# The time mix's residual: added by VectorE from SBUF, instead of by TensorE in PSUM

## The chip, the cores and the metric

The kernel runs on one core of one Trainium2 chip. The time is that of the device, in microseconds (us), as the median of several runs. TensorE multiplies matrices into PSUM, VectorE, ScalarE and GpSimd work element by element, and SyncE (SP) issues the transfers; GpSimd has only tiles in SBUF to work on here. The profile shortens the names: PE is TensorE, PEld its weight loads, DVE VectorE, ACT ScalarE, POOL GpSimd.

## The reference, cut to what matters

Sixteen sequences of 512 tokens with 128 features go through four layers, each with its residual and a layer norm behind it: a recurrent block (time mix and channel mix), a tree of soft decisions, a causal attention with 16 heads of 8, and a mixture of 16 experts of which each token uses two. The change lies in the first block:

```python
x = _ln(x, ln0_g, ln0_b)
xn = _ln(x, pre_g, pre_b)
...
rwkv = jax.nn.sigmoid(r) * (wkv / (wk + K_EPS))
x = x + rwkv @ tm_Wo
xn = _ln(x, post_g, post_b)
...
x = x + (jax.nn.sigmoid(xr @ cm_Wr) + kv)
```

Everything behind the block is a layer norm, so the kernel may keep x centred (its mean over the features taken away).

## The kernel before, in words

A tile is 128 features by 512 tokens in f32: one sequence ("batch"), with the features on the partitions. Means over the features are products with constant matrices: `centre` takes the mean away, `mean_w` gives the mean of the squares. A norm is thus a product with `centre`, a square on ScalarE, a product with `mean_w`, a logarithm and an exponential on ScalarE (together the power -1/2, called r), and one multiplication.

For each batch b, `front(b)` goes from the input to the tensors of the attention. It centres x0 into a PSUM bank (p0). x1 is p0 times g and r, on VectorE, without the bias b of the first norm. A second bank, p1, takes `centre` x x1 and then the centred bias: `b0p` (three bf16 parts of the bias, made in `prepare_mixes`) times a row of ones. `shifted_norm` squares p1, makes r, and writes xn from p1 and r on VectorE; dx is the difference of neighbouring tokens (GpSimd), xx the shifted copy (ScalarE), and three mixes of them follow on VectorE. Four `rwkv` chunks then run the recurrence (scans and a reciprocal on VectorE, products on GpSimd) and leave `rw`. The bank p2 takes `centre` x x1 and the bias rows once more, and over them the four products of `tm_o` and `rw`: that is the new residual x2. ScalarE copies p2 to SBUF as x2 (the tile `y`), while `shifted_norm` reads p2 itself. Then follow the channel mix (`hidden`), the bank p3, the tree (`gates`, `lp`), the rotation for the attention (tile `four`, event "rot") and the transfer out of the parts.

Beside the fronts run long pieces that go through all batches: `operands` (transfers), `greatest` (scores `sc` and their greatest value on VectorE, then small steps on GpSimd), `weighted` (scores `st`, exponentials on ScalarE), `sums` (`o`), `ends`, `gating`, `by_gate` (`us`: products with the gates on GpSimd), `experts` (`acc`) and `output`.

All instructions are written out by a planner, the class `Plan`. Each piece is a generator; the planner keeps a clock and a cost for each engine, and when an engine is free it takes the waiting piece with the smallest (time of asking + slack). The tables `S_FRONT`, `S_RWKV` and so on hold these slacks for TensorE (PE), VectorE (V), ScalarE (A) and GpSimd (G): the larger the number, the later the piece's turn. The order that comes out is each engine's program; on the chip the engines only wait for data and for buffers. `front(b)` starts behind the events "summed" of batch b-1, "mixed" and "normed" of batch b-2, and not before `PERIOD * b - LEAD`. x2 of batch b stands behind "rot" of batch b-1. `W` is VectorE too, at a cost in the plan that grows while GpSimd is busy; `V` is VectorE at the plain cost. PSUM has eight banks, which `bank` takes and `give` returns.

Since nearly all instructions are issued in one helper, the profile shows them under one line, L219, and they are told apart by the names of tiles: `p` is p0 to p3, `x` is x0 and x1, `y` is x2 and later tensors.

Of the kernel before, what the change touches and what calls it, by code (L numbers as in the profile page):

```python
# [18 lines left out]
NC4 = 4  # L19
# [21 lines left out]
HAND_OVER = 0.2  # L41
BANKS = 8
SCORES = 5
PERIOD = 100.0

S_FRONT = {"PE": -6.0, "V": -6.0, "A": 0.0, "G": -20.0}
S_RWKV = {"PE": -10.0, "V": 15.0, "A": -10.0, "G": 6.0}
S_GREATEST = {"PE": -30.0, "V": -3.0, "A": -3.0, "G": -30.0}
S_WEIGHTED = {"PE": -20.0, "A": 30.0, "G": -15.0}
S_SUMS = {"PE": 15.0}  # L50
S_ENDS = {"PE": 6.0, "V": -6.0, "A": 50.0, "G": -15.0}
S_GATE = {"PE": -20.0, "V": 6.0, "A": 6.0, "G": 0.0}
S_EXPERTS = {"PE": 20.0}
FREE = {}
LEAD = 60.0
RWKV_PACE = 5.0
EXPERT_PACE = 0.0
MAX_PACE = 0.0
EXP_PACE = 0.0

# [197 lines left out]
def rwkv_tree_attn_moe(ctx: ExitStack, tc: tile.TileContext, a: dict, out: bass.AP):  # L258
# [54 lines left out]
    def fixed(name, shape, dtype=F32):  # L313
        return const.tile(shape, dtype, tag=name, name=name)
# [25 lines left out]
    def col(i):  # L340
        return vec[:, i:i + 1]
# [23 lines left out]
        if scale != 1.0:  # L365
            V.tensor_scalar(w, w, scale, None, ALU.mult)

    ones, b0p, minus = fixed("ones", [PARTS, T], BF16), fixed("b0p", [PARTS, D], BF16), fixed("minus", [128, 2])
    decay, first = fixed("decay", [128, NC4]), fixed("first", [128, NC4])

    def prepare_mixes():

        V.memset(ones, 1.0)
        b0 = pp.tile([128, PARTS], F32, tag="b0", name="b0")
        for i in range(PARTS):
            V.tensor_copy(b0[:, i:i + 1], col(V_LN0B))
        yield
        p = yield from bank("p_b0")
        mm(p[0:PARTS, 0:D], b0, centre, start=True, stop=True)

        act(decay, vec[:, V_DECAY:V_DECAY + 4], AF.Exp)
        act(decay, decay, AF.Exp, scale=-1.0)
        act(first, vec[:, V_FIRST:V_FIRST + 4], AF.Exp)

        V.tensor_scalar(minus[:, 0:1], col(V_PREB), -1.0, None, ALU.mult)
        V.tensor_scalar(minus[:, 1:2], col(V_POSTB), -1.0, None, ALU.mult)
        yield
        b0r = pp.tile([PARTS, D], F32, tag="b0r", name="b0r")
        V.tensor_copy(b0r, p[0:PARTS, 0:D])
        give(p)  # L390
        b0m = pp.tile([PARTS, D], BF16, tag="b0m", name="b0m")
        for i in range(PARTS):
            V.tensor_copy(b0m, b0r)
            V.tensor_tensor(b0r, b0r, b0m, ALU.subtract)
            if i == 0:
                V.tensor_scalar(b0p, b0m, ident[0:PARTS, 0:1], None, ALU.mult)
            else:
                V.scalar_tensor_tensor(b0p, b0m, ident[0:PARTS, i:i + 1], b0p, ALU.mult, ALU.add)
        event("mixes").set()
        yield 12.0  # L400
        centred(tm_o, 0.5)
        centred(cm_v, 0.5)
        event("outputs").set()
# [131 lines left out]
    def give(p):  # L535
        banks.put(held.pop(id(p))[1])
# [17 lines left out]
        act(r, r, AF.Exp, scale=-0.5)  # L554
        return r

    def variance(d, tag):

        sq = t512(tag)
        act(sq, d, AF.Square)  # L560
        yield
        pv = yield from bank("pv")
        mm(pv, mean_w, sq, start=True, stop=True)
        yield
        return pv

    def normed(d, tag, to):
        pv = yield from variance(d, tag)
        r = rstd_of(pv, ln_eps, to)
        give(pv)  # L570
        yield
        return r

    def front(b, keep):
# [16 lines left out]
        give(p)  # L591
        yield

        def shifted_norm(p, g, minus_b, b):

            r = yield from normed(p, sq, rr)
            shift = yield shifts
            xn = pp.tile([128, T + 1], F32, tag="xn", name="xn")
            G.tensor_copy(xn[:, 0:1], minus_b)
            V.scalar_tensor_tensor(xn[:, 1:T + 1], p, g, r, ALU.mult, ALU.mult)  # L600
            give(p)
            yield
            dx, xx = t512("dx"), t512("xx")
            act(xx, xn[:, 0:T], AF.Identity, bias=b)
            G.tensor_tensor(dx, xn[:, 1:T + 1], xn[:, 0:T], ALU.subtract)
            yield
            return dx, xx, shift
# [5 lines left out]

        yield event("mixes")
        p = yield from bank("p1")
        mm(p, centre, x1, start=True, stop=False)
        mm(p, b0p, ones, start=False, stop=True)
        yield
        dx, xx, shift = yield from shifted_norm(p, col(V_PREG), minus[:, 0:1], col(V_PREB))
        xk, xr, xv = mix(dx, xx, V_MK, "xk"), mix(dx, xx, V_MR, "xr"), mix(dx, xx, V_MV, "xv")  # L620
        shifts.put(shift)
        yield
# [48 lines left out]
        yield event("outputs")  # L671
        yield event("rw", b, 0)
        p = yield from bank("p2")
        mm(p, centre, x1, start=True, stop=False)
        mm(p, b0p, ones, start=False, stop=False)
        event("x1", b).set()
        for c in range(NC4):
            yield event("rw", b, c)
            mm(p, tm_o[:, c, :], rw[:, c, :], start=False, stop=(c == NC4 - 1))
        event("summed", b).set()  # L680
        yield
        if b:
            yield event("rot", b - 1)
        x2 = t512("y")
        copy(x2, p)
        dx, xx, shift = yield from shifted_norm(p, col(V_POSTG), minus[:, 1:2], col(V_POSTB))
        xk, xr = mix(dx, xx, V_CMK, "ck"), mix(dx, xx, V_CMR, "cr")
        shifts.put(shift)
        yield
# [500 lines left out]
```

## Time and profile before

| | |
|---|---|
| runs | 1847.95 us median of 3 (1846.07 to 1852.24) |
| the profiled execution | 1852.02 us, span 1850.2 us |
| mean granted TensorE clock | 0.957 |
| x1 of batches 1, 4, 8, 12 and 15 written at | 82, 359, 759, 1177 and 1495 us |
| p2 of batch 12 complete, rotation of batch 11 done, x2 of batch 12 begun | 1252.5, 1276.9, 1276.1 us |
| last exponential of the attention done | about 1787 us |

A group's row gives the engine, the operation, out<-in, the shapes and the count; then the busy time in us and the mean of one in ns; then the engine's idle time just before these instructions and what ended it. A row of busy time by stretch gives the stretch and its length, then for PE, PEld, DVE, ACT and POOL the busy time and the number of instructions, then the granted clock, the share of the DMA engines and GB/s. A row in order of time gives the start, the time until the end of the last of the merged instructions, and the engine; a TensorE instruction's listed end is modelled, so the start of the next one tells how long it held the engine. An f32 product of 512 columns is two records.

### The profile page before, as it was taken

The numbers are of one execution on the slowest core, as the hardware profiler recorded it, in microseconds if no ns is written. First come the engines' busy times: TensorE is split into PE (matmuls) and PEld (weight loads), VectorE is DVE, ScalarE is ACT, GpSimd is POOL, SyncE is SP. The second block draws the span as 40 slices with busy tenths as digits, with TensorE's granted clock in tenths as the row PEclk, the third lists the DMA queues.
The fourth block names the chain that finished last, engine by engine and source line by source line (L and its number), as shares of the span: only waits on it lengthen the run. The fifth ranks groups of instructions, "written<-read, shape, count | busy, mean of one in ns | idle before, by whom it ended". The sixth has DMA issues, their size and how long they took to land.

```text
span 1850.2 us, 25410 instructions
## 1 busy us (share of the span) xinstructions
PE 1667.9 (90%) x8580; PEld 784.5 (42%) x8668; DVE 1367.0 (74%) x1917; ACT 1172.0 (63%) x1974; POOL 1063.3 (57%) x1329
## 2 busy tenths in 40 slices
PE   5577889899999999899999999999899999998875
PEld 2233434344444444444444444444344444454431
DVE  7695879688888778686887788796878868555512
ACT  3345677668677576667767676767667666765440
POOL 2344544556765747566565757675666757545342
PEclk9687999899999999999999999999999999999996
DMA  3001010221413122222313132222213131233322
GB/s 103 1 6 56 20 38 27 79 79 32 132 37 112 62 91 78 66 82 73 97 46 105 62 96 78 95 67 65 74 58 116 51 107 62 61 94 111 97 80 97
DMA packets 61970, 133.78 MB, mean 72 GB/s; under 512 B 11708, under 2 KB 32974, under 8 KB 61585
## 3 DMA queue, kind: packets, MB, share of 16 engines
q1 hardware_dynamic: 61841, 132.16, 22.6%
q8 instruction: 69, 1.13, 0.2%
q14 instruction: 60, 0.49, 0.1%
HBM read 114.01 MB, written 17.31 MB: 71 GB/s over the span
## 4 chain that ended last, share of the span: by engine, by line
PE 49%; DVE 25%; POOL 11%; issue 6%; ACT 4%; DMA 2%; SPq 1%; POOLq 0%; DVEq 0%; ACTq 0%
PE acc L219 8%; PE sc L219 7%; PE st L219 6%; DVE sk L219 6%; PE o L219 5%; DVE skv L219 5%; PE p L219 5%; PE pv L219 4%; DVE nmx L219 3%; PE pr L219 2%; PE ph L219 2%; POOL us L219 2%; PE pk L219 2%; POOL lp L219 2%; PE pvv L219 2%
## 5 line engine op out<-in xcount | busy, mean ns | idle before, releaser
L219 DVE TENSOR_REDUCE nmx<-sc 128x1 f32<-128x384 f32 (+3 forms) x704 | 433.8, 634 | 195.6 <-PE sc L219 148.4
L219 ACT ACTIVATE ew<-st 128x512 f32<-128x512 f32 (+1 forms) x704 | 382.3, 556 | 252.1 <-PE st L219 248.0
L219 POOL TENSOR_TENSOR us<-u,gb 128x512 f32<-128x512 f32 x248 | 328.5, 1334 | 159.3 <-PE acc L219 83.6
L219 PE MATMUL acc<-us,w_mo 128*128 128x512 f32 x512 | 277.7, 634 | 17.0 <-POOL us L219 16.7
L219 PE MATMUL st<-qop,kop 128*128 128x512 bf16 (+1 forms) x1018 | 253.9, 304 | 18.1 <-DMA qop<-rows 8.5
L219 PE MATMUL sc<-kop,qop 128*128 128x128 bf16 x1021 | 257.4, 305 | 11.3 <-DVE nmx L219 7.5
L219 DVE RECIPROCAL sk<-sk 128x512 f32<-128x512 f32 x64 | 213.8, 3341 | 0.0
L219 PE MATMUL o<-ew,vaug 128*32 128x512 f32 (+3 forms) x2048 | 193.8, 447 | 6.6 <-ACT ew L219 3.4
L219 POOL TENSOR_TENSOR sk<-fk,sk 128x512 f32<-128x512 f32 x64 | 102.2, 1597 | 142.2 <-DVE sk L219 123.3
L219 PEld LDWEIGHTS <-qop 128*128 128x128 bf16 x1024 | 94.1, 100 | 182.8 <-issue 158.7
L219 PE MATMUL st<-idents,masks 128*128 128x128 bf16 (+2 forms) x673 | 161.7, 240 | 0.6 <-issue 0.4
L219 PE MATMUL sc<-masks,idents 128*128 128x128 bf16 (+2 forms) x656 | 154.9, 236 | 0.3 <-issue 0.2
L219 PEld LDWEIGHTS <-kop 128*128 128x128 bf16 x1024 | 91.6, 99 | 146.7 <-issue 102.5
L219 POOL TENSOR_TENSOR skv<-t,skv 128x512 f32<-128x512 f32 x64 | 81.4, 1272 | 89.1 <-DVE skv L219 84.3
L219 POOL TENSOR_TENSOR rw<-skv,sk 128x512 f32<-128x512 f32 x64 | 86.8, 1357 | 64.5 <-DVE sk L219 61.0
L219 PEld LDWEIGHTS acc<-us,w_mo 128*128 128x128 f32 x512 | 84.1, 195 | 80.7 <-issue 42.1
L219 POOL TENSOR_TENSOR lp<-gates,lp 128x8 f32<-128x8 f32 (+6 forms) x224 | 115.2, 536 | 2.7
L219 DVE TENSOR_TENSOR_SCAN skv<-decay,kv 128x511 f32<-128x511 f32 x64 | 112.7, 1761 | 0.0
L219 PEld LDWEIGHTS <-idents 128*128 128x128 bf16 x704 | 69.8, 99 | 88.8 <-issue 82.9
L219 PE MATMUL pv<-sq,mean_w 128*128 128x512 f32 x160 | 93.2, 666 | 14.3 <-ACT sq L219 13.5
L219 PE MATMUL p<-rw,w_tm 128*128 128x512 f32 x128 | 74.3, 664 | 34.9 <-POOL rw L219 34.5
L219 ACT ACTIVATE r<-pv,eps 128x512 f32<-128x512 f32 x96 | 65.9, 687 | 52.9 <-PE pv L219 30.1
(213 smaller groups left out, 3120.6 us busy)
## 6 DMA issues: line engine op xcount, KB each, us to landing
gb<-gd SPq DMA_DIRECT2D x128, 512.0 KB
qop<-there SPq DMA_DIRECT2D x576, 32.0 KB
kop<-there SPq DMA_DIRECT2D x192, 96.0 KB
there<-parts SPq DMA_DIRECT2D x32, 384.0 KB
x<-xT SPq DMA_DIRECT2D x16, 256.0 KB
out<-sqb SPq DMA_DIRECT2D x16, 256.0 KB
qop<-rows SPq DMA_DIRECT2D x192, 4.0 KB
w_mo<-w_mo SPq DMA_DIRECT2D x1, 1160.0 KB
```

The lines of the kernel that those rows point to most:

```text
L219: ins = getattr(self.engine, op)(out, *args, **kw)
```

## The change

The bias of the first norm is centred once into a column, `cb0`, in `prepare_mixes`; the row of ones, the three bf16 parts and the work that makes them go. p1 takes only `centre` x x1. ScalarE writes p1 plus `cb0` over x1 in SBUF, and the bank is given back at once; `shifted_norm` then reads x1 from SBUF. p2 takes only the four products of `tm_o` and `rw`; VectorE adds x1 to it as it writes x2, and `shifted_norm` reads x2 from SBUF. xn is now planned at the cost of `W`. The event "summed" is set behind that addition; the event "x1", for which no piece waits, goes. The planner's period, nine slacks and two paces get other values.

```diff
-PERIOD = 100.0
+PERIOD = 96.0
-S_FRONT = {"PE": -6.0, "V": -6.0, "A": 0.0, "G": -20.0}
-S_RWKV = {"PE": -10.0, "V": 15.0, "A": -10.0, "G": 6.0}
-S_GREATEST = {"PE": -30.0, "V": -3.0, "A": -3.0, "G": -30.0}
-S_WEIGHTED = {"PE": -20.0, "A": 30.0, "G": -15.0}
+S_FRONT = {"PE": -6.0, "V": -6.0, "A": 0.0, "G": 0.0}
+S_RWKV = {"PE": -10.0, "V": 20.0, "A": -30.0, "G": 6.0}
+S_GREATEST = {"PE": -30.0, "V": -3.0, "A": -3.0, "G": -3.0}
+S_WEIGHTED = {"PE": -20.0, "A": 3.0, "G": -10.0}
-S_ENDS = {"PE": 6.0, "V": -6.0, "A": 50.0, "G": -15.0}
-S_GATE = {"PE": -20.0, "V": 6.0, "A": 6.0, "G": 0.0}
+S_ENDS = {"PE": 6.0, "V": -3.0, "A": 30.0, "G": -15.0}
+S_GATE = {"PE": -20.0, "V": 6.0, "A": 6.0, "G": 30.0}
-RWKV_PACE = 5.0
-EXPERT_PACE = 0.0
+RWKV_PACE = 7.0
+EXPERT_PACE = 1.0
...
     def prepare_mixes():
-        V.memset(ones, 1.0)
-        b0 = pp.tile([128, PARTS], F32, tag="b0", name="b0")
-        for i in range(PARTS):
-            V.tensor_copy(b0[:, i:i + 1], col(V_LN0B))
-        yield
         p = yield from bank("p_b0")
-        mm(p[0:PARTS, 0:D], b0, centre, start=True, stop=True)
+        mm(p[:, 0:2], centre, vec[:, V_LN0B:V_LN0B + 2], start=True, stop=True)
...
-        b0r = pp.tile([PARTS, D], F32, tag="b0r", name="b0r")
-        V.tensor_copy(b0r, p[0:PARTS, 0:D])
+        V.tensor_copy(cb0, p[:, 0:1])
         give(p)
-        b0m = pp.tile([PARTS, D], BF16, tag="b0m", name="b0m")
-        for i in range(PARTS):
...
-    def variance(d, tag):
+    def variance(d, tag, bias=0.0):
         sq = t512(tag)
-        act(sq, d, AF.Square)
+        act(sq, d, AF.Square, bias=bias)
...
-            V.scalar_tensor_tensor(xn[:, 1:T + 1], p, g, r, ALU.mult, ALU.mult)
-            give(p)
+            W.scalar_tensor_tensor(xn[:, 1:T + 1], x, g, r, ALU.mult, ALU.mult)
...
-        mm(p, centre, x1, start=True, stop=False)
-        mm(p, b0p, ones, start=False, stop=True)
-        yield
-        dx, xx, shift = yield from shifted_norm(p, col(V_PREG), minus[:, 0:1], col(V_PREB))
+        mm(p, centre, x1, start=True, stop=True)
+        yield
+        act(x1, p, AF.Identity, bias=cb0)
+        give(p)
+        dx, xx, shift = yield from shifted_norm(x1, col(V_PREG), minus[:, 0:1], col(V_PREB))
...
         p = yield from bank("p2")
-        mm(p, centre, x1, start=True, stop=False)
-        mm(p, b0p, ones, start=False, stop=False)
-        event("x1", b).set()
         for c in range(NC4):
             yield event("rw", b, c)
-            mm(p, tm_o[:, c, :], rw[:, c, :], start=False, stop=(c == NC4 - 1))
-        event("summed", b).set()
+            mm(p, tm_o[:, c, :], rw[:, c, :], start=(c == 0), stop=(c == NC4 - 1))
         yield
         if b:
             yield event("rot", b - 1)
         x2 = t512("y")
-        copy(x2, p)
-        dx, xx, shift = yield from shifted_norm(p, col(V_POSTG), minus[:, 1:2], col(V_POSTB))
+        V.tensor_tensor(x2, p, x1, ALU.add)
+        event("summed", b).set()
+        give(p)
+        dx, xx, shift = yield from shifted_norm(x2, col(V_POSTG), minus[:, 1:2], col(V_POSTB))
```

More of the change, by code (lines that the diff above doesn't have):

```diff
@@ L366, in centred @@
             V.tensor_scalar(w, w, scale, None, ALU.mult)
-    ones, b0p, minus = fixed("ones", [PARTS, T], BF16), fixed("b0p", [PARTS, D], BF16), fixed("minus", [128, 2])
+    cb0, minus = fixed("cb0", [128, 1]), fixed("minus", [128, 2])
     decay, first = fixed("decay", [128, NC4]), fixed("first", [128, NC4])
     def prepare_mixes():
-        V.memset(ones, 1.0)
-        b0 = pp.tile([128, PARTS], F32, tag="b0", name="b0")
-        for i in range(PARTS):
-            V.tensor_copy(b0[:, i:i + 1], col(V_LN0B))
-        yield
         p = yield from bank("p_b0")
-        mm(p[0:PARTS, 0:D], b0, centre, start=True, stop=True)
+        mm(p[:, 0:2], centre, vec[:, V_LN0B:V_LN0B + 2], start=True, stop=True)
         act(decay, vec[:, V_DECAY:V_DECAY + 4], AF.Exp)
@@ L387, in prepare_mixes @@
         yield
-        b0r = pp.tile([PARTS, D], F32, tag="b0r", name="b0r")
-        V.tensor_copy(b0r, p[0:PARTS, 0:D])
+        V.tensor_copy(cb0, p[:, 0:1])
         give(p)
-        b0m = pp.tile([PARTS, D], BF16, tag="b0m", name="b0m")
-        for i in range(PARTS):
[L393 to L398, printed above, removed]
         event("mixes").set()
@@ L592, in front, with shifted_norm @@
         yield
-        def shifted_norm(p, g, minus_b, b):
-            r = yield from normed(p, sq, rr)
+        def shifted_norm(x, g, minus_b, b):
+            r = yield from normed(x, sq, rr)
             shift = yield shifts
```

## The prediction

> **What bounds the kernel now.** I read the busy shares first, then the busy time by stretch, then the chain that ended last, then TensorE in order of time, and last the groups and tiles that the change touches.
>
> ```profile
> PE 1667.9 (90%) x8580; PEld 784.5 (42%) x8668; DVE 1367.0 (74%) x1917; ACT 1172.0 (63%) x1974; POOL 1063.3 (57%) x1329
> ```
> ```profile
> 0.00:300.00 300.00, 216.57 (x763) 94.95 (x770) 226.95 (x298) 157.02 (x247) 129.34 (x182) 0.86 0.12 37
> 300.00:1500.00 1200.00, 1150.58 (x6146) 545.81 (x6209) 959.04 (x1315) 833.08 (x1410) 764.30 (x950) 0.99 0.24 76
> ```
> ```profile
> PE 49%; DVE 25%; POOL 11%; issue 6%; ACT 4%; DMA 2%; SPq 1%; POOLq 0%; DVEq 0%; ACTq 0%
> ```
>
> The mean of 90% hides three stages. From 300 to 1500 us TensorE is busy 1150.6 of 1200 us (96%) at a granted clock of 0.99, and nothing else is near: VectorE 80%, ScalarE 69%, GpSimd 64%. There TensorE is the bound. In the first 300 us it is idle for 83 us, because the first batches' chain runs through VectorE. The third stage begins when the last exponentials are done (about 1787): 60 us of short dependent steps, which the change doesn't touch. About half the last-ending chain is TensorE, in many lines. So a TensorE instruction removed after about 300 us should be worth the time until the next matmul can start, and one removed before it next to nothing.
>
> What a matmul is worth is its start-to-start step, not its listed 0.59 us, since matmuls overlap. In order of time, TensorE alone:
>
> ```profile
> 1012.41 0.22 PE L219 MATMUL st<-idents,masks 128*128 128x128 bf16 x1
> 1012.47 1.08 PE L219 MATMUL p<-x,centre 128*128 128x512 f32 x2
> 1013.48 0.39 PE L219 MATMUL p<-ones,b0p 3*128 3x512 bf16 x1
> 1013.79 0.39 PE L219 MATMUL st<-qop,kop 128*128 128x512 bf16 x1
> ```
>
> The f32 product of x1 (two records) holds the engine from 1012.47 to 1013.48, 1.01 us; the three bias rows from 1013.48 to 1013.79, 0.31 us.
>
> **The change part by part.**
>
> *Removed from TensorE.* Per batch: in p2 the centring product and the bias rows (1.01 + 0.31 = 1.32 us), in p1 the bias rows (0.31 us). After 300 us there are p2 of batches 3 to 15 and p1 of batches 4 to 15: 13 x 1.32 + 12 x 0.31 = 20.9 us. What falls before 300 us lies in TensorE's idle time and counts as nothing.
>
> *Removed at the start.* The ones memset, the copies of b0 and the splitting into three bf16 parts, some 3 us of VectorE before 11 us. The split ends at 10.75 us, when r, which x1 needs, had ended at 10.67: worth 0.1 us. Nothing.
>
> *Moved and added.* These rows price it:
>
> ```profile
> L219 ACT COPY y<-p 128x512 f32<-128x512 f32 x16 | 9.3, 581 | 17.5 <-PE p L219 17.5
> L219 ACT ACTIVATE sq<-y 128x512 f32<-128x512 f32 x16 | 10.1, 628 | 31.7 <-DVE y L219 31.7
> L219 DVE TENSOR_TENSOR att<-z,pw 128x512 f32<-128x512 f32 x16 | 10.7, 666 | 4.1 <-PE pw L219 3.7
> L219 DVE SCALAR_TENSOR_TENSOR xn<-p,vec,r 128x512 f32<-128x512 f32 x32 | 23.9, 746 | 22.8 <-ACT r L219 22.7
> ```
>
> ScalarE gains an Identity out of PSUM with a bias column (nearest row: the squares out of PSUM, 600 ns) and loses the copy of x2 (581): 16 x 0.02, nothing. Its 32 squares now read SBUF: 628 against 600, +0.9 us over the run. VectorE gains the addition of x1 to p2, one operand in PSUM and one in SBUF, as att has it: 16 x 0.67 = 10.7 us. All this lies beside a TensorE that is busy 96%: on VectorE it is 0.67 of about 103 us a batch, from 80% to 81%. Were that cover gone it would cost its full 11 us.
>
> *xn now reads SBUF twice* (x and r), in place of PSUM and SBUF. Duration ns min/median/max of tiles with two SBUF inputs:
>
> ```profile
> L219 DVE SCALAR_TENSOR_TENSOR xn<-p,vec,r x32: 737/744/753, 18.3 to 1600.6; 128x512 f32<-128x512 f32 x32
> L219 DVE SCALAR_TENSOR_TENSOR xk<-dx,vec,xx x16: 741/752/1743, 23.4 to 1508.8; 128x512 f32<-128x512 f32 x16
> L219 DVE SCALAR_TENSOR_TENSOR ck<-dx,vec,xx x16: 742/1140/2603, 79.7 to 1604.6; 128x512 f32<-128x512 f32 x16
> ```
>
> xn never exceeds 753 ns; the others reach 1743 and 2603. [...] the low end is the same 740 ns, the high end is longer by about one GpSimd product (1.27 us). By the mean of xk (1066 ns) the 32 xn cost 32 x 0.32 = 10 us[...]. [...] VectorE thus ends near 82%, still covered.
>
> *On the path of the first batches*, where latency counts: p1 loses 0.31 us, then gains the Identity (0.60) ahead of its square; p2's addition replaces a copy (+0.09); two xn at +0.32 each; two squares from SBUF (+0.06): about +1.1 us a batch, for three batches +3 us.
>
> *The moved event.* "summed" was set when p2 was complete; now it is set behind the addition, which stands behind the wait for "rot" of the batch before. The next batch's front stands behind it: its x load on SP's queue, its first product, all of its chain. For batches 12 and 13 the trace has:
>
> ```profile
> 1251.42 1.08 PE L219 MATMUL p<-rw,w_tm 128*128 128x512 f32 x2
> 1275.57 1.28 POOL L219 TENSOR_TENSOR four<-four 128x512 f32<-128x512 f32 x1
> 1276.09 0.58 ACT L219 COPY y<-p 128x512 f32<-128x512 f32 x1
> 1278.82 0.75 DVE L219 SCALAR_TENSOR_TENSOR x<-p,vec,r 128x512 f32<-128x512 f32 x1 [2.86 <-ACT r L219]
> ```
>
> p2 of batch 12 was complete at 1252.5; the rotation of batch 11 held x2 back to 1276.1; x1 of batch 13 came 2.7 us later, 6.2 us behind its own first product at 1272.67. Under the new order it comes after x2 plus 0.7 (addition), 4 (the code's pause for the load) and 6.2, so some 8 us later. From x1 to the end of p2 it takes 76 to 90 us over batches 2 to 13, about 79 in the middle, so the new loop is 11 + 79 + 1 = 91 us against a spacing of 102 to 103: it fits, with 11 us to spare, and costs nothing. The load itself was issued at 1207, 65 us ahead of its use, so its later place in SP's queue is covered too.
>
> *Slacks, paces, period.* The planner's order changes everywhere: on GpSimd the gate products go from 0 to +30 and the greatest scores from -30 to -3, on ScalarE the exponentials from +30 to +3 and the time mix from -10 to -30; TensorE's own values stay. No row prices a reordering. From below: it could recover at most the 49 us of TensorE's idle time between 300 and 1500, half of it at a guess, -25. From above: if its idle share doubled on half of that stretch, +25. I take 0, as TensorE's work is the same in any order. The period of 100 hardly binds now (the last x1 stand 102, 108 and 108 us apart: 1176.8, 1278.8, 1387.0, 1495.1), so 96 should change little.
>
> **Sum.** -20.9 + 3 + 0 = -18 us. The profiled execution took 1852.0 us (span 1850.2 and 1.8 around it), which gives 1834; the median of the runs is 4 us below it, so 1847.95 - 18 = **1830 us**.
>
> **Rivals.**
> *The order packs better too.* For: VectorE waits 148 us for sc, ScalarE 248 us for st, so buffers turn late; p1's PSUM bank is given back earlier. Against: only 49 us are to be had. At half of it, 1830 - 25 = 1805.
> *Hidden anyway.* From batch 3 on x2 starts within 2 us of the rotation of the batch before, so the loop x2 to rotation (95 to 110 us) also has the period. If its waits for VectorE, ScalarE and GpSimd set it, TensorE only idles more: the 18 us vanish, within 0.3%, 1843 to 1853. Against: alone, batch 0 needs 79 us for that loop; the rest is queueing, mostly at TensorE.
> *Slower: the loop through "summed" becomes the bound.* Place: x2, next front, time mix, p2. It decides once x1 to p2's end exceeds 91 us; batch 4 has 89.8 now, xn and the Identity add 1 to 2, and the pace of 7 between chunks may delay the last by 6. At a period of 105 instead of 103.4, 13 x 1.6 = 21 us more: 1869.
>
> **How the numbers follow.** Forecast 0.43, better packing 0.14, hidden 0.13, loop 0.30. A measurement of this kernel tells about 0.3% (5.5 us) from no change. Faster is 0.43 + 0.14 = 0.57, same 0.13, slower 0.30. The forecast's own range is 1820 to 1841. The range that leaves out 2 in 10 reaches half-way into the packing case and up to about the loop's price: 1808 to 1868.
>
> **What would show it.** TensorE's busy time falls by some 26 us (16 x 1.63), its share from 300 to 1500 stays near 96%, and fronts come some 101.8 us apart. xn spreads to a mean near 1.05 us with a top over 1.7. x1 follows x2 of the batch before by about 11 us, and p2 still ends ahead of the rotation. The forecast is wrong if TensorE's idle share in that stretch grows by over 2 points (loop or order), or if x2 now waits for p2 rather than for the rotation.

## The result, and the profile after

The changed kernel takes 1859.34 us (median of 5 runs, 1857.42 to 1860.6); the kernel before took 1846.61 us in the same comparison. The ratio is 1.0058, with a 95% interval of 1.0042 to 1.0073: slower by 0.58%, some 11 to 13 us. The forecast was 1830, with a range of 1820 to 1841.

The page of the kernel after, busy shares first:

```profile
PE 1647.7 (89%) x8604; PEld 778.8 (42%) x8604; DVE 1384.3 (75%) x1920; ACT 1180.6 (64%) x1978; POOL 1069.3 (58%) x1329
```

Busy time by stretch, the same stretches as in the prediction:

```profile
0.00:300.00 300.00, 209.16 (x738) 92.50 (x738) 227.93 (x290) 163.21 (x253) 124.11 (x182) 0.87 0.11 36
300.00:1500.00 1200.00, 1127.97 (x6126) 539.66 (x6119) 966.35 (x1314) 826.23 (x1396) 771.45 (x941) 0.98 0.24 75
```

The chain that ended last, by engine:

```profile
PE 51%; DVE 24%; POOL 10%; ACT 5%; issue 5%; DMA 4%; SPq 1%; DVEq 0%; POOLq 0%; ACTq 0%
```

TensorE's work fell as intended, from 1667.9 to 1647.7 us. But from 300 to 1500 us it is now busy 94% instead of 96%: its idle time there grew from 49.4 to 72.0 us. Work went, and idle time took its place. TensorE still has the largest share in both summaries above; only the order of time shows what it waits for.

The instructions that the change added or touched, as groups of one shape each:

```profile
L219 ACT ACTIVATE x<-p,cb 128x512 f32<-128x512 f32 x16 | 11.0, 688 | 6.7 <-PE p L219 6.6
L219 DVE TENSOR_TENSOR y<-p,x 128x512 f32<-128x512 f32 x16 | 10.9, 683 | 5.2 <-PE p L219 5.2
L219 ACT ACTIVATE sq<-x 128x512 f32<-128x512 f32 x16 | 10.1, 630 | 0.5
```

And xn, in the tile's own rows (duration ns min/median/max):

```profile
L219 DVE SCALAR_TENSOR_TENSOR xn<-x,vec,r x16: 742/750/755, 18.2 to 1522.3; 128x512 f32<-128x512 f32 x16
L219 DVE SCALAR_TENSOR_TENSOR xn<-y,vec,r x16: 742/745/752, 78.2 to 1609.2; 128x512 f32<-128x512 f32 x16
```

All of this is within 0.1 us of its price, or below it (xn). As busy time, none of it explains 12 us. So I split the run at the points where x2 is begun (the tile `y`, the row y<-p,x after and y<-p before):

| | before | after | difference so far |
|---|---|---|---|
| x2 of batch 3 | 344 | 339 | -5 |
| x2 of batch 6 | 651 | 664 | +13 |
| x2 of batch 15 | 1591.5 | 1601.7 | +10 |
| end of the span | 1850 | 1857 | +7 |

The profiled execution of before took 1852.0 us, 5 us over the median of its runs; that of after is the median itself. So the end of the span shows 7 us where the medians differ by 12.7. In the traces of three other runs in before's order (less TensorE work, no gating chain, gates of the batch before, all below) the stretch from batch 3 to 6 agrees with this one within 1.4 us.

There are two losses. One is made in batches 3 to 6: +18 us, where the first batches had already gained 5. The other is a gain that doesn't come: over the nine batches from 6 to 15, where nine times 1.6 us of TensorE's work is gone, the new kernel is only 3 us quicker.

Busy time by stretch before, then after, cut at 660 us:

```profile
300.00:660.00 360.00, 344.26 (x1846) 163.70 (x1864) 295.61 (x407) 249.13 (x423) 220.49 (x278) 0.98 0.23 69
660.00:1500.00 840.00, 806.32 (x4301) 382.11 (x4345) 663.42 (x909) 583.96 (x988) 543.81 (x672) 0.99 0.25 79
```
```profile
300.00:660.00 360.00, 331.53 (x1812) 158.41 (x1804) 277.92 (x381) 243.87 (x414) 229.18 (x271) 0.98 0.22 70
660.00:1500.00 840.00, 796.45 (x4316) 381.26 (x4315) 688.43 (x934) 582.36 (x984) 542.27 (x671) 0.98 0.25 77
```

TensorE's idle time grew by 12.7 us in the first stretch (15.7 to 28.5) and by 9.9 us in the second (33.7 to 43.6).

**What TensorE waits for in the second stretch.** Its waits from 700 to 1400 us in the kernel after (us in total, times, longest):

```profile
PE pg L219 <- DVE gaug L219: 22.2, 7, 3.2
PE pmx L219 <- POOL nm L219: 8.7, 9, 1.5
```

In the kernel before, the same stretch has:

```profile
PE pg L219 <- DVE gaug L219: 1.1, 1, 1.1
```

`pg` are four small transposes of the gates; `gaug` is the last of a chain of small VectorE instructions in `gating` that choose two experts for each token. In the order of time, VectorE first (start, us until the end):

```profile
1178.22 0.24 DVE L219 RECIPROCAL rec<-pot 128x16 f32<-128x16 f32 x1
...
1179.28 0.22 DVE L219 TENSOR_TENSOR m<-m,v 128x64 f32<-128x64 f32 x1
1179.54 1.19 DVE L219 TENSOR_TENSOR m<-m,tab 128x64 f32<-128x64 f32 x1
1180.76 0.22 DVE L219 TENSOR_REDUCE v<-m 128x4 f32<-128x64 f32 x1
1181.02 1.79 DVE L219 TENSOR_TENSOR s<-tab,v 128x64 f32<-128x64 f32 x1
1182.84 0.23 DVE L219 TENSOR_TENSOR s<-s,s 128x64 f32<-128x64 f32 x1
1183.10 0.23 DVE L219 TENSOR_TENSOR gaug<-s,e 128x64 f32<-128x64 f32 x1
1183.24 0.68 DVE L219 TENSOR_TENSOR y<-p,x 128x512 f32<-128x512 f32 x1
```

GpSimd in the same microseconds:

```profile
1176.35 1.26 POOL L219 TENSOR_TENSOR four<-four 128x512 f32<-128x512 f32 x1
...
1179.38 1.27 POOL L219 TENSOR_TENSOR us<-u,gb 128x512 f32<-128x512 f32 x1
1180.60 2.12 POOL L219 TENSOR_TENSOR four<-four,parts 128x1024 f32<-128x1024 f32 x1
```

And TensorE:

```profile
1183.47 1.01 PE L219 MATMUL pg<-ident,gaug 128*16 128x128 f32 x4 [3.17 <-DVE gaug L219]
1184.28 0.63 PE L219 MATMUL sc<-kop,qop 128*128 128x128 bf16 x4
1184.70 0.63 PE L219 MATMUL sc<-masks,idents 128*128 128x512 bf16 x1
```

Two instructions of 64 columns, 0.22 us each at their shortest, take 1.19 and 1.79 us. Each began just behind a GpSimd product (1179.54 behind 1179.38, 1181.02 behind 1180.60), and they ended 0.08 and 0.09 us after those products did. Between the two the reduction `v<-m`, which reads one tile, took 0.22 us beside the second product (1180.76), and none of its 48 took over 0.221 us. The prediction had looked for long instructions of this kind at xn; they stand at another place. TensorE stood for 3.17 us until the chain was through. Behind the chain VectorE has x2 as well: the rotation had ended at 1177.6 and x2 began at 1183.24, 5.6 us later.

x2 reads nothing of the rotation; the planner only puts it behind. In before it began between 1.4 us ahead of the rotation's end and 1.7 us behind it (batches 3 to 15; batch 12 at 1276.1, with the rotation's end at 1276.9). So the lateness measures x2's place in an engine's order, and not a wait for data.

The stop comes with half speed. The busy times of two stretches from its end on:

```profile
1183.00:1189.00 6.00, 5.53 (x22) 2.96 (x22) 2.27 (x5) 4.01 (x7) 1.11 (x1) 0.50 0.03 8
1189.00:1195.00 6.00, 6.00 (x46) 3.05 (x46) 4.31 (x8) 4.96 (x10) 2.19 (x3) 1.00 0.60 194
```

The granted clock is 0.50 for 6 us: 22 instructions where the next 6 us have 46. The time from the last matmul's start to pg is 3.4 us in nine batches one after the other (pg at 765 to 1602 us), and at eight of these stops, all but the one at 1498, the clock went to 0.50 for 3.4 or 6.8 us. Shorter stops had it too: before, those of 2.2, 2.2 and 2.5 us ahead of pg (at 966, 1485 and 1593 us) had 3.4 us of half clock each. One of 5.8 us, ahead of `acc` at 784 us, had 6.8 us of it. From what length on a stop brings it was not shown. From 660 to 1600 us the trace of after has 30.7 us at half clock, that of before 20.5.

From batch 7 on the kernel after repeats itself, nearly to the tenth: x2 5.6 us behind the rotation of the batch before, and from x2 to the next rotation 99.1 us, together the spacing of 104.7. Before, it was 0.1 and 103.8 us, together 103.9 (means over batches 8 to 14). So the loop from x2 to the rotation did become 4.7 us shorter, and 5.5 us were put in front of it.

### The profile page after: what moved, and what is told of

Same layout as the page of the kernel before. It is cut to its first block, busy times and chain, and to the rows that moved or that the text cites. A ratio compares the mean times of both kernels' runs of the same rounds, so it can differ in the third digit from the quotient of the medians.

```text
span 1857.5 us, 25315 instructions
## 1 busy us (share of the span) xinstructions
PE 1647.7 (89%) x8604; PEld 778.8 (42%) x8604; DVE 1384.3 (75%) x1920; ACT 1180.6 (64%) x1978; POOL 1069.3 (58%) x1329
## 4 chain that ended last, share of the span: by engine, by line
PE 51%; DVE 24%; POOL 10%; ACT 5%; issue 5%; DMA 4%; SPq 1%; DVEq 0%; POOLq 0%; ACTq 0%
PE acc L219 8%; PE sc L219 7%; PE p L219 7%; PE st L219 6%; DVE skv L219 6%; PE pv L219 4%; PE o L219 4%; DVE sk L219 4%; POOL us L219 3%; DVE nmx L219 3%; PE pr L219 2%; DMA gb<-gd 2%; PE ph L219 2%; DVE m L219 2%; DVE s L219 2%
## 5 line engine op out<-in xcount | busy, mean ns | idle before, releaser
L219 DVE TENSOR_REDUCE nmx<-sc 128x1 f32<-128x384 f32 (+3 forms) x704 | 438.4, 636 | 188.2 <-PE sc L219 183.7
L219 POOL TENSOR_TENSOR us<-u,gb 128x512 f32<-128x512 f32 x248 | 324.7, 1317 | 186.4 <-PE acc L219 103.9
L219 PE MATMUL acc<-us,w_mo 128*128 128x512 f32 x512 | 270.2, 621 | 15.1 <-POOL us L219 15.1
L219 PE MATMUL st<-qop,kop 128*128 128x512 bf16 (+3 forms) x1024 | 256.1, 304 | 13.9 <-DMA qop<-rows 10.0
L219 PE MATMUL sc<-kop,qop 128*128 128x128 bf16 (+3 forms) x1024 | 259.8, 307 | 2.2 <-DVE m L219 0.9
L219 PE MATMUL o<-ew,vaug 128*32 128x512 f32 (+3 forms) x2048 | 187.1, 444 | 0.1
L219 POOL TENSOR_TENSOR sk<-fk,sk 128x512 f32<-128x512 f32 x64 | 106.8, 1668 | 124.9 <-ACT gates L219 61.1
L219 PE MATMUL sc<-masks,idents 128*128 128x128 bf16 (+2 forms) x704 | 175.2, 249 | 0.0
L219 PE MATMUL st<-idents,masks 128*128 128x128 bf16 (+2 forms) x704 | 173.7, 247 | 0.0
L219 POOL TENSOR_TENSOR rw<-skv,sk 128x512 f32<-128x512 f32 x64 | 92.9, 1452 | 35.2 <-DVE sk L219 26.8
L219 POOL TENSOR_TENSOR dx<-xn 128x512 f32<-128x512 f32 x32 | 33.1, 1035 | 125.5 <-DVE xn L219 125.5
```

The costliest lines, as they stand in the source:

```text
L219: ins = getattr(self.engine, op)(out, *args, **kw)
```

## The experiments

Every run's ratio is against the kernel before on the same chip, with its 95% interval. "Spacing" is the mean distance of x2 from batch 8 to 14, "lateness" is x2's start behind the end of the rotation of the batch before, "step" the time from the start of the matmul ahead of pg to pg (mean over the pg from 865 to 1600 us). Names: *after* and *before* are the two kernels.

| run | us | ratio | spacing | lateness | step |
|---|---|---|---|---|---|
| before | 1846.6 | 1 | 103.9 | 0.1 | 1.4 |
| after | 1859.3 | 1.0058 | 104.7 | 5.6 | 3.4 |
| short gating chain in after | 1839.1 | 0.9934 | 102.9 | 4.3 | 2.3 |
| no gating chain in after | 1806.2 | 0.9761 | 100.0 | -0.1 | 0.1 |
| no gating chain in before | 1812.1 | 0.9813 | 101.6 | 0.0 | 0.1 |
| x2 by ScalarE in after | 1870.7 | 1.0114 | 105.5 | 1.5 | 3.4 |
| gates of the batch before in after | 1852.3 | 1.0013 | 104.7 | 5.6 | 0.1 |
| both of these | 1837.0 | 0.9926 | 101.8 | 1.5 | 0.1 |

### Is TensorE's saved work worth anything?

In the order of before, the centring product and the bias rows were left out, and nothing else moved:

```diff
-        mm(p, centre, x1, start=True, stop=False)
-        mm(p, b0p, ones, start=False, stop=True)
+        mm(p, centre, x1, start=True, stop=True)
...
-            mm(p, tm_o[:, c, :], rw[:, c, :], start=False, stop=(c == NC4 - 1))
+            mm(p, tm_o[:, c, :], rw[:, c, :], start=(c == 0), stop=(c == NC4 - 1))
```

> The kernel before, in its own order; left out are the bias rows of p1 and p2 and the centring product in p2, so that the residual and a bias are missing from the result; nothing is put in their place. Prediction's term (TensorE is the bound after 300 us): 20.9 us less, 1822-1830. Rival B (hidden; the loop of waits sets the pace): 1843-1850.

Measured: 1834.33 us, ratio 0.9913 (0.989 to 0.9935), 16 us less than before (12 to 20 by the interval). In before's order TensorE's work is worth about four fifths of the 20.9 us of the forecast. The term was right in kind, and the loss lies elsewhere.

And the other half of the pair, VectorE copying x2 in the order of before, with nothing taken from TensorE:

```diff
-        copy(x2, p)
+        with tc.issue_after(plan.last["V"].ins):
+            plan.last["V"] = nc.vector.tensor_copy(x2, p)
```

> The kernel before, in its own planned order, only that VectorE instead of ScalarE copies p2 as x2. Theory A: x2 then stands behind VectorE's work of the moment, the gating chain in some batches, 1 to 3 us late, 5-25 us more in all: 1852-1872. If the engine of x2 is of no account: 1844-1850.

Measured: 1859.07 us, ratio 1.0045 (1.003 to 1.006). The move of x2 to VectorE alone costs 8 us. In the forecast it cost nothing, since VectorE was busy only 80% of the time. In batches 3 to 7 x2 now begins 0.8 to 2.4 us behind the rotation's end, where ScalarE's copy had begun between 1.4 us ahead of it and 0.3 us behind; just ahead of it on VectorE stand instructions of the chain of gating, or greatest scores (`nmx`). By batch 6 x2 is 14 us later than in before, and hardly more after that.

### Is it the chain of gating?

In the order of after, four instructions of the chain (those that read the ranks) became memsets at the same places of VectorE's order:

```diff
-                V.tensor_tensor(m, m, ranks, ALU.mult)
+                in_place_of("V", vector_us("tensor_tensor", m), nc.vector, "memset", m, 1.0)
...
-                V.tensor_tensor(s, ranks, over_e(v1), ALU.is_equal)
+                in_place_of("V", vector_us("tensor_tensor", s), nc.vector, "memset", s, 0.5)
```

> The kernel after, every engine's order unchanged; in the gating's VectorE chain the two products with the ranks and the two comparisons with the ranks are replaced by memsets of the same tiles (the choice of experts is thereby left out and the result is not the reference's). Theory A (the gating chain, slowed by GpSimd, makes the pg transposes on TensorE and the addition of x1 behind it on VectorE late, once in every batch): the wait of pg falls from 3.4 us to under 0.5, x2 follows the rotation within 2 us instead of 5.6, the spacing of x2 falls from 104.5 to 100-101 us, the time to 1820-1832. Rival B (the loop from x2 to the rotation has its own length, whatever pg and x2 wait for): spacing 104 or more, 1852-1860.

Measured: 1839.09 us, ratio 0.9934 (0.9909 to 0.9959): 20 us less than after, though above the 1820 to 1832 expected. The step fell from 3.4 to 2.3 us only, because the next two instructions of the chain, `s` and `gaug`, now met the same two GpSimd products and took 1.16 and 2.04 us (at 1169.6 and 1170.8). So all the chain's instructions with two inputs were replaced in the same way (two of the six edits shown):

```diff
-                V.tensor_tensor(m, x, over_e(v1), ALU.is_equal)
+                in_place_of("V", vector_us("tensor_tensor", m), nc.vector, "memset", m, 1.0)
...
-            V.tensor_tensor(gate, s1, e, ALU.mult)
+            in_place_of("V", vector_us("tensor_tensor", gate), nc.vector, "memset", gate, 0.1)
```

> The kernel after, order unchanged; every two-input VectorE instruction of the gating's choice of experts (behind the softmax) is now a memset of its tile, so that the choice is left out and the result is not the reference's. Theory A' (TensorE is the bound, and what the change lost are TensorE's stop at pg and the half clock behind it): pg's step falls to 0.5 us or less in all middle batches, the half clock between 300 and 1600 us from 44 to under 20 us, spacing 99.5 to 101 us, 1810-1825. Rival (the loop through x2 has its own length): spacing stays at 102.8 as in the first experiment, 1835-1842.

Measured: 1806.18 us, ratio 0.9761 (0.9725 to 0.9796). Without the chain the spacing is 100.0 us, with no lateness and no step. The control is the same edit in before:

> The control of the fifth experiment: the kernel before, its order unchanged, with the same memsets in place of the gating's two-input VectorE instructions (the choice of experts is left out, the result is not the reference's). If the late gating chain is what the new order suffers from and the old one mostly does not (its steps before pg sum to some 14 us in batches 6 to 13, those of after to 31 over nine batches): 15-20 us less than before, 1828-1835, against the 53 us less that after gained. If it is as dear in the old order: 1795-1805.

Measured: 1812.14 us, ratio 0.9813 (0.979 to 0.9836). This missed: before has the chain's price too, 35 us where some 15 were expected. So the chain doesn't cost 53 us because of the change; it costs 53 us after and 35 us before. The difference, 18 us, is the change's. And without the chain in either, after is the faster kernel, some 6 us in these medians (1806.2 against 1812.1) or 0.5%, 10 us, by the two ratios. The chain thus decides which of the two kernels is the faster.

The traces split it as before. Without the chain, after still loses 18 us on before between batches 3 and 6 (x2 from 337 to 660 us against 344 to 649), but over the nine batches that follow it is 22 us quicker, where with the chain it is 3 us quicker. So 19 us of the missing gain are the chain's, and the 18 us of batches 3 to 6 are not.

How the chain's instructions are caught differs between the two orders. Tile rows of before, then of after (duration ns min/median/max):

```profile
L219 DVE TENSOR_TENSOR m<-m,tab x32: 224/225/2053, 344.9 to 1807.8; 128x64 f32<-128x64 f32 x32
...
L219 DVE TENSOR_TENSOR s<-tab,v x32: 224/226/1184, 345.4 to 1808.3; 128x64 f32<-128x64 f32 x32
```
```profile
L219 DVE TENSOR_TENSOR m<-m,tab x32: 224/1189/1203, 331.2 to 1815.3; 128x64 f32<-128x64 f32 x32
...
L219 DVE TENSOR_TENSOR s<-tab,v x32: 224/1056/1791, 331.7 to 1815.8; 128x64 f32<-128x64 f32 x32
```

Before, the median is the undisturbed 225 ns; after, more than half of them are caught: from batch 7 on the order repeats itself, and `s` stands with 1.79 us just ahead of `s`, `gaug` and x2 in every batch. Over the run the chain's two-input instructions took 54 us more than at their shortest after, and 32 us more before.

### Which wait behind the chain: TensorE's, x2's, or VectorE's own time?

First x2 was taken away from behind the chain: in the order of after, ScalarE copies it, and the centring product is back in p2 (0.95 us a batch more for TensorE, an estimate of the expectation below).

```diff
+        in_place_of("PE", 0.0, nc.tensor, "matmul", p, centre, x1, start=False, stop=True)
...
-        V.tensor_tensor(x2, p, x1, ALU.add)
+        with tc.issue_after(plan.last["A"].ins):
+            plan.last["A"] = nc.scalar.copy(x2, p)
```

> The kernel after, in the same planned order, but the centring product of x1 goes back into p2 (as its last product) and ScalarE copies p2 as x2 at the place of the addition. If x2's wait on VectorE behind the gating chain sets the pace: x2 follows the rotation within 1 us, the spacing falls by some 4 us to about 100.5, the time to 1822-1835 although TensorE has 0.95 us a batch more to do. If TensorE's stop at pg and the half clock after it set the pace: pg still waits 3 us or more, spacing 104-105.5, 1855-1875.

Measured: 1870.68 us, ratio 1.0114 (1.0087 to 1.014). The lateness fell from 5.6 to 1.5 us, but the loop to the next rotation grew from 99.1 to 104.0 us, and nothing was gained. TensorE's waits from 700 to 1400 us still begin with pg:

```profile
PE pg L219 <- DVE gaug L219: 19.0, 6, 3.2
```

I took this to mean that TensorE's stop was the whole cause, and that was wrong. The next run takes only the stop away: the transposes read the gate tile of the batch before, so they needn't wait, while the whole chain and x2 behind it stay.

```diff
-                tr(pg[0:NE, t * 128:(t + 1) * 128], gaug[:, t, :], ident)
+                tr(pg[0:NE, t * 128:(t + 1) * 128], gaugs[(b - 1) % 2 if b else 0][:, t, :], ident)
```

> The kernel after with one operand changed: TensorE's transposes of the gates read the gate tile of the batch before, so the experts are weighted with the gates of the batch before. VectorE's whole chain of gating stays, and x2 stays behind it; only TensorE's wait for the chain goes. Theory (TensorE's stop of 3.4 us a batch, and the half clock behind it, is what the chain costs in the new order): the step ahead of pg falls to 0.5 us or less, x2 still starts about 5 us behind the rotation, the spacing of x2 falls from 104.7 to 100 to 102 us, and the run takes 1815 to 1835 us. Rival (VectorE's occupation by the chain, and x2 late behind it, is the cost): the step goes as well, but the spacing stays at 104 to 105 us and the run at 1850 to 1860 us.

Measured: 1852.31 us, ratio 1.0013 (1.0002 to 1.0024), spacing unchanged at 104.7 us; x2 of batch 15 begins at 1602 us as in after, so what little was gained lies behind it. My theory fell; the rival's numbers came. The waits of this run, same window:

```profile
PE sc L219 <- DVE y L219: 16.6, 7, 2.4
PE pmx L219 <- POOL nm L219: 7.1, 8, 1.0
PE pv L219 <- ACT rows L219: 4.2, 7, 0.6
```

The 22.2 us ahead of pg are gone, and 16.6 us of a new wait stand there: `sc`, a few matmuls later, now stops for `y`, that is for x2 behind the same chain. (It reads nothing of x2; what x2 sets free is p2's PSUM bank, which `sc` can be waiting for.) The stops are now 2.75 us from start to start, and the half clock from 660 to 1600 us is 37.5 us, more than with the stop at pg. That left two readings: two waits side by side, either of which holds the pace, or VectorE's own time in the chain. One run with both edits tells them apart, for it keeps the chain and takes both waits:

> The kernel after with both earlier edits at once: ScalarE copies x2 out of the bank (the centring product back in it), and the transposes of the gates read the tile of the batch before (the experts are weighted with those). VectorE's whole chain stays; neither TensorE's transposes nor x2 wait for it. Theory (two waits side by side, either of which holds the pace): step ahead of pg 0.3 us or less, x2 1.5 us behind the rotation, spacing 100 to 102.5 us, 1820 to 1842 us, although each edit alone gave 1871 and 1852. Rival (VectorE's occupation): spacing 104 us and more, 1850 to 1872 us.

Measured: 1836.98 us, ratio 0.9926 (0.9897 to 0.9954), spacing 101.8 us. Against after, the edits alone are worth +0.6% and -0.4%; together they are worth -1.3%. The chain is as slow as ever in this run, as the tile's row shows:

```profile
L219 DVE TENSOR_TENSOR m<-m,tab x32: 224/1194/1332, 337.6 to 1798.4; 128x64 f32<-128x64 f32 x32
```

but nothing waits for it on TensorE from 700 to 1400 us:

```profile
PE pmx L219 <- POOL nm L219: 13.4, 13, 2.7
PE pr L219 <- DVE nmx L219: 3.0, 6, 0.5
```

and the half clock from 660 to 1600 us fell from 30.7 to 3.4 us. So for the pace it is two waits side by side: with only x2's taken away the spacing is 105.5 us, with only TensorE's 104.7, and with both gone it falls to 101.8. They aren't the chain's whole price: the run without the chain is 31 us faster still, and at most some 15 us of that (16 x 0.95) are the centring product that stands in this run. What the rest is, VectorE's own time in the chain perhaps, no run shows.

The control in before, gates of the batch before:

> The same one operand changed in the kernel before (the experts are weighted with the gates of the batch before). Its steps ahead of pg sum to some 20 us over the run, against some 47 us in after. Theory: it gains less than after does, 8 to 20 us (1827 to 1840 us), and the two kernels without the wait stand with after the faster by 5 to 15 us. Rival: no gain beyond 0.3% here either.

Measured: 1838.14 us, ratio 0.9943 (0.9926 to 0.996). The size came as expected, the rest didn't: with this edit in both, after is the slower one, by 0.7%. And the gain isn't in the loop: x2 of batch 15 begins at 1591 us with and without the edit, and only what follows it is shorter, 244 us instead of 259, as the last batch's stop of 5.7 us ahead of pg is gone and the half clock after 1600 us fell from 46 to 28 us. (Some of these 15 us may be the 5 us by which before's profiled execution was slow.) Of the 35 us that the chain costs before, the pace between the x2 is thus not explained by TensorE's wait.

### Can the order take both waits away?

The same two waits were attacked with nothing left out. First only the transposes were issued later, by 8 and by 14 TensorE instructions; their copy and transfer follow them.

```diff
-            for t in range(NT):
-                tr(pg[0:NE, t * 128:(t + 1) * 128], gaug[:, t, :], ident)
+            late = [14, [transposes], False, held[id(pg)][1]]
+            plan.late.append(late)
```

> The kernel after, nothing left out: the four transposes of the gates, and ScalarE's copy of them and the transfer that follows, are issued 8 TensorE instructions later than in after; every other instruction keeps its place. Eight instructions are some 2 us of TensorE's work. Theory: the step ahead of pg falls from 3.4 to about 1.5 us, and the spacing by as much, with less half clock: 1830 to 1848 us. Rival: no change, 1855 to 1862 us, as VectorE's chain sets the pace.

Measured: 1864.96 us, ratio 1.0083 (1.0051 to 1.0115).

> The same with 14 TensorE instructions, some 3.3 us of its work. Theory: the step ahead of pg falls to 0.5 us or less and the half clock between 300 and 1600 us from 44 to about 25 us; spacing 100 to 102 us, 1815 to 1838 us, faster than the kernel before. Rival: no change, 1855 to 1862 us.

Measured: 1886.03 us, ratio 1.0199 (1.0182 to 1.0217). The step fell to 2.7 and 0.9 us, and the time rose. The waits of the second of these show the exchange again:

```profile
PE sc L234 <- DVE y L234: 16.8, 6, 2.8
PE pmx L234 <- POOL nm L234: 14.6, 12, 2.7
```

With x2 moved ahead of VectorE's second choice too:

> The kernel after, nothing left out, two moves in the order of issue: VectorE's eight instructions of the second choice of the gating stand behind the addition of x2 where they stood just ahead of it, and the four transposes of the gates, with their copy and transfer, 14 TensorE instructions later. Theory of the two waits: x2 about 1 us behind the rotation, step ahead of pg 1 us or less, spacing 101 to 103 us, 1825 to 1845 us (the moved transposes alone gave 1886). Rival: 1860 to 1890 us, as with the moved transposes alone.

Measured: 1858.51 us, ratio 1.0036 (1.0024 to 1.0049). x2's lateness is 1.2 us, but the chain, now behind x2, ends later, and the step is 2.2 us again. It is 28 us better than the moved transposes alone, as two waits side by side would have it, yet no better than before.

### Are the new slacks to blame?

The slacks, paces and period were exchanged between the two programs: after with before's, and before with after's.

```diff
-PERIOD = 96.0
+PERIOD = 100.0
...
-S_GATE = {"PE": -20.0, "V": 6.0, "A": 6.0, "G": 30.0}
+S_GATE = {"PE": -20.0, "V": 6.0, "A": 6.0, "G": 0.0}
```

> The kernel after with the period, slacks and paces of before. If the new slacks alone made it slower: 1825-1838, as in the third experiment plus a little. If slacks fit only the program that they were made for, and every other pairing gives an order with stops of its own: 1855-1900.

Measured: 1892.2 us, ratio 1.0223 (1.0174 to 1.0272).

> The kernel before with the period, slacks and paces of after. If the new slacks are bad in themselves: 1860-1875, some 12-25 us above before as after is. If they fit only the program that they were made for: 1855-1900 here too, and then this run and the one with old slacks on the new program are both slower than after.

Measured: 1885.75 us, ratio 1.0189 (1.0149 to 1.0229). Each set suits only its own program; the exchanges cost 33 and 39 us. So "undo the slacks" is not a part that can be undone alone, and the order can weigh twice as much as the 16 us of work that the change removes.

Then new orders were looked for. The planner's own clock (it comes from its cost table when the kernel is built) ends at 1812.1 us for before and 1795.1 for after, so the planner, like me, saw a gain of 17 us. In all three new sets the chain's instructions were planned as waiting for GpSimd:

```diff
+    def behind(op, out, *args):
+        return 0.23 + 0.7 * min(1.3, max(0.0, plan.free.get("G", 0.0) - max(plan.now, plan.free.get("V", 0.0))))
...
-                V.tensor_tensor(m, m, ranks, ALU.mult)
+                H.tensor_tensor(m, m, ranks, ALU.mult)
```

> The kernel after, nothing left out; the planner charges the gating's two-input VectorE instructions 0.23 us plus 0.7 of the time that GpSimd is still busy (at most 1.3), and period, slacks and paces are drawn anew for this cost by the length of the plan. If the change was lost by an order that trusts too short a gating chain: pg's step under 1 us in most batches and 1825-1845, better than both. If any order loses as much somewhere else: 1850-1870.

Measured: 1981.36 us, ratio 1.072 (1.0701 to 1.0739), though the planner had ended it at 1797.7. TensorE's waits over the whole of that run:

```profile
PE p L219 <- POOL rw L219: 72.0, 19, 10.2
PE pk L219 <- DVE xk L219: 64.4, 12, 6.5
PE pv L219 <- ACT sq L219: 53.6, 21, 4.7
```

> As the run before, with a second set of period, slacks and paces of nearly the same planned length (2.6 us more). Same expectation, 1828-1848; the difference of the two runs shows how far a planned length tells the time.

Measured: 1845.13 us, ratio 0.9984 (0.997 to 0.9999), planned at 1800.3. This is after's program, 14 us better than after and level with before.

> The kernel before (product and bias rows on TensorE, x2 by ScalarE) with the same cost for the gating and period, slacks and paces drawn anew in the same way; planned length 0.6 to 3.2 us over those of the two runs before. If the edit itself is worth its 1.6 us of TensorE a batch once the order is mended: 10-20 us slower than those two, 1845-1860. If the order decides all: within 8 us of them.

Measured: 1877.22 us, ratio 1.0155 (1.0135 to 1.0174), planned at 1800.9. Three plans within 3.2 us of each other took 1845, 1877 and 1981 us: the plan's length says nothing here about such differences. It had the sign right for the two exchanges, whose plans end at 1845.5 (after with before's slacks) and 1829.3 us.

Last, the two moves (x2 ahead, transposes later) in the order that stood level with before:

> The order of the second new set of slacks (1845 us), nothing left out, with the two moves in it: x2's addition ahead of VectorE's second choice of the gating where it stood one or two instructions behind it, and the transposes of the gates 12 TensorE instructions later. Theory of the two waits: step ahead of pg 0.5 us or less instead of 2.0 to 2.7, x2 1 to 2 us behind the rotation in every batch instead of 6.2 in every second one, mean spacing 100 to 101.5 us instead of 102.4, 1822 to 1838 us. Rival (the moved transposes are late for the experts, as in the run with these moved alone): 1850 us and more.

Measured: 1889.2 us, ratio 1.0221 (1.0207 to 1.0235). x2's lateness is 0.8 to 1.2 us from batch 6 on as meant, but the step is 4.0 us in every second batch, and 44 us from 660 to 1600 us are at half clock where that order had none. Of the versions that leave nothing out, none is more than 0.2% faster than before.

## Why the prediction was wrong, point by point

**The step that failed** is the one on slacks, paces and period: "I take 0, as TensorE's work is the same in any order". The work is the same; the stops aren't. Its bounds, -25 and +25 us, were worked from TensorE's idle time and were of the right kind: the idle time from 300 to 1500 us grew by 22.6 us. What I left out of the sum was what stands ahead of pg and of x2 on VectorE. The price of it, from the runs with and without the chain, is 19 us over batches 6 to 15; a further 18 us are lost in batches 3 to 6. Together they outweigh the 16 us of TensorE's saved work and the 5 us gained before batch 3.

The forecast's own signs of being wrong did not come. TensorE's idle share from 300 to 1500 us grew by 1.9 points (4.1 to 6.0%), just under the 2 points named, and x2 didn't wait for p2. Busy time fell by 20 us where some 26 were forecast.

**Removed from TensorE, -20.9**: right in kind, -16 when done alone in before's order.

**"On VectorE from 80% to 81% ... covered"**: the share came true (966 of 1200 us), the cover didn't. VectorE's copy alone cost 8 us in before's order. This is a second step that failed: the term was put at nothing from a mean load. With x2 on VectorE, x2 stands behind the chain of gating from batch 7 on, 5.6 us behind the rotation; on ScalarE it had been 0.1 us behind on average. A mean load of 80% didn't tell the wait of this one instruction.

**xn, +10 and covered**: too dear. It never exceeds 755 ns. GpSimd was mostly waiting for xn itself at that point: it was at work during only 4 of the 32, and its idle time ahead of dx shows the wait, 125.5 us in all where it was 61.7 before (page of after):

```profile
L219 POOL TENSOR_TENSOR dx<-xn 128x512 f32<-128x512 f32 x32 | 33.1, 1035 | 125.5 <-DVE xn L219 125.5
```

The long cases among the instructions with two SBUF inputs (`xk` up to 1743 ns, `ck` up to 2603 before) were right to weigh, but they were weighed only for the instructions that the change turned into readers of two SBUF tiles. The ones that were long in every batch from 7 on after the change (1.19 and 1.79 us in place of 0.22) were in another piece, with 64 columns each, and had always read two.

**Identity on ScalarE, 600**: measured 688 ns; 1.4 us over the run. **The addition of x1, 666**: measured 683.

**The loop through "summed", 91 us, with 11 to spare**: right. x1 of batch 13 came 12.0 us behind x2 of batch 12 (1300.45 against 1288.41), and p2 was still complete 17 us ahead of x2. The rival built on this loop had the right sign and a time, 1869, within 10 us of the measured one, by luck: its reason is not there. ("The rotation of batch 11 held x2 back to 1276.1" was a misreading, as the rotation ended at 1276.9. It changed no sum.)

**The rival "hidden anyway"** named the loop from x2 to the rotation, which has the period: 99.1 us in after, plus the 5.6 in front. But in before's order the saved work did show (16 us), so it was not hidden as that rival had it.

**The first batches, +3**: x2 of batch 3 came 5 us earlier, not later.

**Left open.** What costs 18 us in batches 3 to 6. From x2 of batch 3 to x2 of batch 6 TensorE is idle for 22.0 us after and 8.9 before, and busy for 302.4 and 297.6 us. So 13 us are standing time, of which a wait for a transfer (`st` for `qop`, 5.1 us) and one for `us` (2.4 us) are the longest; the other 5 us are work, although three batches of the change take some 5 us away. Both runs without the chain keep the difference, so it isn't the chain's. All thirteen traces of the changed program, under four sets of slacks, have 321 to 333 us there, and all seven of the program before, under three, have 305 to 320; so neither do the slacks alone explain it. VectorE's copy of x2 alone, in before's order, adds 9 us there. No run took the loss out.

Open as well: why the chain costs 35 us before, of which TensorE's wait, taken away, gives back 10 to 12; and what the Identity on ScalarE and the moved event cost, which were not run alone.

## What to carry to other kernels

Before an instruction goes to an engine with room to spare, read in order of time what stands ahead of it there and who else waits for that: one slow chain can hold two consumers, and then taking either wait away gains next to nothing (-7 and +11 us here, -22 with both), so test them together. Where a planner writes the order anew, price the change by the stops in the trace and not by the work; its own clock was off by up to 184 us here. Look among the small VectorE instructions too for some that take longer beside GpSimd: here 0.22 us became 1.05 to 1.79, and each ended within 0.1 us after a GpSimd instruction.

## What the hardware showed that I had not expected

- A VectorE instruction of 64 columns with two SBUF inputs, 0.22 us at its shortest, took 1.19, 1.05 and 1.79 us, and ended within 0.1 us after the GpSimd instruction that was under way when it began. A 512-column xn, which has two SBUF inputs too, was never caught in 32 cases; GpSimd was at work during only 4 of them.
- Stops of 3.4 us on TensorE came with 3.4 or 6.8 us at half clock in eight of nine batches, and stops of 2.2 to 2.5 us (before) had 3.4 us of it too; with both waits gone the half clock fell to 3.4 us in all from 660 to 1600 us.
- Reading PSUM or SBUF made no difference to VectorE's xn: 744 ns before, 745 and 750 ns after.
- A ScalarE Identity with a bias column out of PSUM took 688 ns where a square out of PSUM took 600 (before).
